# Paged attention with a conditional residual on one Trainium2 core: value rows gathered raw and masked on the way into the operand, a fixed opening, and loads in written order

## The chip, the cores and the metric

The kernel runs on one NeuronCore of a Trainium2 chip. The metric is device time in microseconds. It was run three times; the median counts. Beside that, one execution was taken by the hardware profiler, and all readings of engines, waits and transfers come from it.

Five engines work side by side: TensorE (matrix products), VectorE, ScalarE (activations), GpSimd, and SyncE (SP), which here only issues transfers. Each works through its own queue of instructions in order, and semaphores between them carry the dependencies.

## The reference, cut to what matters

```python
# B=64 sequences, S=32 new tokens each, HID=512; D=128, HQ=32 query heads, HK=8 key heads
# 64 pages of 32 keys; 16 pages to a sequence, so L=512 cached positions
x = x + einsum('bct,bcd->bdt', x, L0_weights[cond])        # 32x32 mix picked per sequence
q, k, v = x @ Wq.T, x @ Wk.T, x @ Wv.T
q = rope(rmsnorm(q, q_norm_w), pos); k = rope(rmsnorm(k, k_norm_w), pos)
# pos = cache_seqlens[:, None] + arange(S)
kc = k_cache[block_table]; vc = v_cache[block_table]       # 16 pages in a table's order
k_all, v_all = concat([kc, k]), concat([vc, v])            # 512 cached + 32 new
valid = concat([arange(512) < cache_seqlens, ones(32)])
scores = where(valid, q @ k_all.T / sqrt(D), -1e30)        # 4 query heads share a key head
o = softmax(scores) @ v_all
x = x + o @ Wo.T
```

All of it is float32.

## The kernel before, in words

**Tiling.** A step is a tile of 128 tokens, that is BT = 4 sequences (batches) of 32 tokens. There are 16 steps to a half of the heads (`hh`: 4 key heads, 16 query heads) and two halves, so 32 steps. Within a step there are 16 slots, one for each batch and key head (`slot = bt * GH + g`). In a slot TensorE makes `scores` (four matmuls: 512 cached keys x 128 queries, transposed, so that keys lie on partitions), ScalarE takes exp of them into `pr` without a maximum, and one slot later TensorE makes `values` from `pr` and the value operand `v_t`. That operand has a 129th column of ones for the denominator: a masked position has a zero row there, 129th column included, so masking needs no work on the scores. The new tokens' own keys come in `new_scores` and `new_values` once a step. `turn` transposes a finished batch, and `out_proj` of a step runs in slot 3 of the following one.

**The next step's preparation.** In the slots of one step the next step's tile is prepared by a table of pieces: x with its mix (`x1_a`), its transpose (`x1_b`), the projections of k, v and four groups of q (`k_a`, `v_a`, `q_a`; a projection is four float32 matmuls 512 wide, and `norm_rope` follows on ScalarE, VectorE and GpSimd) and the transposes of the results (`k_b`, `q_b`). They lie in slots 0, 2, 4, 5, 6, ... 15.

**Cached keys.** `load_k` fetches the 16 pages of a batch by 16 transfers on SP, 1 MB in all, two batches ahead; `head_keys` copies one head's keys out of it on VectorE, one batch ahead.

**Cached values.** A table `v_tab` in device memory is built for each half: `table_piece` reads 128 rows of the cache, sets the column of ones and writes 129 columns for each head; a last row is zero. Then `load_v` gathers rows from the table straight into `v_t` (two buffers, `v_bufs`), four gathers of 128 rows to a batch, where `v_idx` points a masked position at the zero row. Only the first four batches (`DIRECT`) are gathered raw and masked by VectorE (L326). The first table is built before the loop, the second in steps 4 to 11.

**Order.** Nearly all of the order is left to a planner, which takes instructions by priority of writing as their operands become ready by its own estimate; so an engine's queue may differ from the order of the source. `tc.issue_after` and `tc.manual_schedule` are the means to fix an order: the first puts instructions behind a given one on its engine, the second keeps the written order for the engines named (all, when none is named).

**Opening.** Weights and Wo are issued on ScalarE's queue; the tables of sine and cosine are made first for one tile (`tables_a`), then for the other 15 in two goes (`tables_b`, `angles`). The main loop follows.

At the end the kernel counts denominators outside a safe range; when there is one, a second, exact version runs (`run(True)`). It did not run here.

Of the kernel before, what the change touches and what calls it, by code (L numbers as in the profile page):

```python
# [48 lines left out]
PIECES = PAGES * PSIZE // P  # L49
ZROW = PAGES * PSIZE  # L50
DIRECT = BT
# [4 lines left out]
def cond_resid_paged_attention_kernel(  # L56
# [29 lines left out]

    cond_sb = const.tile([P, NT], I32, tag="cond", name="cond_sb")
    nc.sync.dma_start(cond_sb, cond)
    pages_sb = const.tile([B, NPP], I32, tag="pages", name="pages_sb")
    nc.sync.dma_start(pages_sb, pages)  # L90
    pages_v_sb = const.tile([P, B * VC], I32, tag="pages_v", name="pages_v_sb")
    nc.sync.dma_start(pages_v_sb, pages_v)
    lens_sb = const.tile([P, NT], I32, tag="lens", name="lens_sb")
    nc.sync.dma_start(lens_sb, lens)
    lens_all_i = const.tile([P, B], I32, tag="lens_all_i", name="lens_all_i")
    nc.sync.dma_start(lens_all_i, lens_row.partition_broadcast(P))

    part_i = const.tile([P, 1], I32, tag="part_i", name="part_i")
    nc.gpsimd.iota(part_i, pattern=[[0, 1]], base=0, channel_multiplier=1)
    row_i = const.tile([P, 1], I32, tag="row_i", name="row_i")  # L100
    nc.vector.tensor_scalar(row_i, part_i, S - 1, None, ALU.bitwise_and)
    row = const.tile([P, 1], F32, tag="row", name="row")
    nc.vector.tensor_copy(row, row_i)
    part = const.tile([P, 1], F32, tag="part", name="part")
    nc.vector.tensor_copy(part, part_i)

    cond_idx = const.tile([P, NT], I32, tag="cond_idx", name="cond_idx")
    nc.vector.tensor_scalar(cond_idx, cond_sb, float(S), row, ALU.mult, ALU.add)

    ident = const.tile([P, P], F32, tag="ident", name="ident")  # L110
    make_identity(nc, ident)


    v_idx = const.tile([P, B, VC], I32, tag="v_idx", name="v_idx")
# [3 lines left out]
    norm_w = {}  # L118
    for name, src in (("q", qn_w), ("k", kn_w)):
        w = const.tile([P, D], F32, tag=f"norm_{name}", name=f"norm_{name}")  # L120
        norm_w[name] = w, src
    freq = const.tile([P, HD], F32, tag="freq", name="freq")
# [8 lines left out]
    def angles(t0, t1, tmp):  # L131

        n = (t1 - t0) * HD
        ang, turns, red = (tmp[:, i, 0:n] for i in range(3))
        for t in range(t0, t1):
            nc.vector.tensor_scalar(
                ang[:, (t - t0) * HD : (t - t0 + 1) * HD],
                freq,
                pos[:, t : t + 1],
                None,  # L140
                ALU.mult,
            )
# [16 lines left out]
    def tables_a(tmp):  # L159

        for name in norm_w:
            w, src = norm_w[name]
            nc.sync.dma_start(w, src.partition_broadcast(P))
            norm_w[name] = w
        nc.sync.dma_start(freq, inv_freq.partition_broadcast(P))
        nc.vector.memset(half_pi, math.pi / 2)
        nc.vector.memset(minus_half, -0.5)
        nc.vector.tensor_copy(pos, lens_sb)
        nc.vector.tensor_scalar(pos, pos, row, None, ALU.add)
        angles(0, 1, tmp)  # L170

    def gather_rows(at):
        nc.vector.tensor_copy(lens_all, lens_all_i)
        for c in range(VC):
            key = const.tile([P, 1], F32, tag=f"key{c}", name=f"key{c}")
            nc.vector.tensor_scalar_add(key, part, float(c * P))
            nc.vector.tensor_scalar(valid[:, :, c], lens_all, key, None, ALU.is_gt)
        row2 = const.tile([P, 1], F32, tag="row2", name="row2")
        nc.vector.tensor_scalar(row2, row, float(NHH), None, ALU.mult)
        nc.vector.tensor_scalar(  # L180
            v_row, pages_v_sb, float(PSIZE * NHH), row2, ALU.mult, ALU.add
        )
        past = const.tile([P, 1], F32, tag="past", name="past")
        nc.vector.tensor_scalar_add(past, row, -float(ZROW))
        nc.vector.tensor_scalar(at, pages_v_sb, float(PSIZE), past, ALU.mult, ALU.add)
        nc.vector.tensor_tensor(at, at, valid.rearrange("p b c -> p (b c)"), ALU.mult)
        nc.vector.tensor_scalar_add(
            v_idx.rearrange("p b c -> p (b c)"), at, float(ZROW)
        )

    def tables_b(kv):

        for t0, t1 in ((1, NT // 2), (NT // 2, NT)):
            angles(t0, t1, kv.tile([P, 3, 8 * HD], F32, tag="k_t", name=f"trig{t0}"))
# [3 lines left out]
    ]  # L198
    v_tab = [
        dram.tile([ZROW + 1, GH * (D + 1)], F32, tag=f"v_tab{hh}", name=f"v_tab{hh}")  # L200
        for hh in range(NHH)
# [8 lines left out]
    def steps_of(exact, pools):  # L210
# [31 lines left out]


        wt = {}

        def load_w(kind, hh, g=0, eng=None):
# [10 lines left out]
            if kind == "o" and not exact:  # L257
                src = src.rearrange("(h j p) e -> h p j e", h=REP, p=S)
                for h in range(REP):
                    (eng or nc.gpsimd).dma_start(t[h * S : (h + 1) * S, :, :], src[h])  # L260
                return
            (eng or nc.gpsimd).dma_start(t, src.rearrange("(c p) e -> p c e", p=P))

        def load_cond_weights(t):
            w_sel = work.tile([P, S], F32, tag="w_sel", name=f"w_sel_{t}_{uid}")
# [8 lines left out]
        def load_x(t):  # L274
            xt = work.tile([P, HID], F32, tag="acc", name=f"xt_{t}_{uid}", bufs=3)
            nc.sync.dma_start(xt, x[t * P : (t + 1) * P, :])
            return xt, load_cond_weights(t)
# [3 lines left out]
        def load_k(hh, b):  # L281
            k_raw = kv.tile([P, NPP, GH, PSIZE], F32, tag="k_t", name=f"k_t_{hh}_{b}_{uid}")

            with ExitStack() as order:
                if last_k:
                    order.enter_context(tc.issue_after(last_k[0]))
# [15 lines left out]
        def load_v(hh, b):  # L302
            v_t = v_bufs[b % 2]
            if exact or hh or b >= DIRECT:
                for c in range(VC):
                    nc.gpsimd.indirect_dma_start(  # L306
                        out=v_t[:, c, :, :].rearrange("p g d -> p (g d)"),
                        out_offset=None,
                        in_=v_tab[hh],
                        in_offset=bass.IndirectOffsetOnAxis(  # L310
                            ap=v_idx[:, b, c : c + 1], axis=0
                        ),
                    )
                return v_t
            raw = wpool.tile([P, VC, GH * D], F32, tag="wo3", name=f"raw_{b}")
            for c in range(VC):
                nc.gpsimd.indirect_dma_start(
                    out=raw[:, c, :],
                    out_offset=None,
                    in_=vc,  # L320
                    in_offset=bass.IndirectOffsetOnAxis(
                        ap=v_row[:, b * VC + c : b * VC + c + 1], axis=0
                    ),
                )
                ok = valid[:, b, c : c + 1]
                nc.vector.tensor_scalar(  # L326
                    v_t[:, c, :, 0:D],
                    raw[:, c, :].rearrange("p (g d) -> p g d", g=GH),
                    ok,
                    None,  # L330
                    ALU.mult,
                )
# [405 lines left out]
        for g in range(GH):  # L738
            load_w("q", 0, g, eng=nc.scalar)
# [157 lines left out]
```

## Time and profile before

| | |
|---|---|
| time, median of 3 | 2466.02 us (2464.14 to 2476.43) |
| profiled execution, span | 2339.8 us |
| granted TensorE clock, mean | 0.986 |
| transfers | 335.94 MB, mean 144 GB/s |
| landing of a gathered value chunk (256 KB), median | 4.5 us |
| exp of one slot on ScalarE, x512 | 597 ns |
| masked copy on VectorE (first four batches), x16 | 480 ns |
| gather issue on GpSimd, x496 | 1137 ns |

How to read it: the timed runs and the profiled execution are measured apart and differ by a constant-looking 125 us, so a timed run is compared with a timed run and a span with a span. "Busy" of TensorE is the modelled time of pipelined matmuls. Clock is the share of full speed that was granted to TensorE[...]. An instruction's line is the line in the listing above.

### The profile page before, as it was taken

To read this page: it belongs to the slowest core of one execution; us is meant where nothing else is said; L and a number is where in the kernel's file an instruction comes from. 1 tells how busy PE (TensorE), PEld (TensorE's weight loads), DVE (VectorE), ACT (ScalarE), POOL (GpSimd) and SP (SyncE) were. 2 spreads that over 40 slices of the span, in tenths; PEclk is the share of its full clock that TensorE was granted. 3 is DMA by queue.
4 is the path that set the end of the run, shared out by engine and by line. 5 is a ranking of instruction groups with operands and counts; after the bars stand their busy time and mean duration, and the time that the engine had idled before them with its cause. 6 is when DMAs were issued, how large, how long until landed. Compare 5 with 4: busy or idle time off the path is not lost.

```text
span 2339.8 us, 41048 instructions
## 1 busy us (share of the span) xinstructions
PE 2229.0 (95%) x13538; PEld 1565.5 (67%) x13538; DVE 1075.7 (46%) x2800; ACT 611.5 (26%) x1180; POOL 848.4 (36%) x963
## 2 busy tenths in 40 slices
PE   3789999999999999999998999999999999999997
PEld 1466666776666776667775667766667776667775
DVE  4444444554444554444552444544444554444452
ACT  1222222222222322222321222322222232222231
POOL 3133333443333443333443333433333443334341
PEclk8889999999999999999999999999999999999999
DMA  8564555544444544454847355544454544445442
GB/s 255 154 183 139 168 166 166 160 117 122 136 133 141 143 116 122 132 141 136 252 127 195 105 146 144 141 120 124 134 145 141 144 132 121 134 128 149 141 133 60
DMA packets 381155, 335.94 MB, mean 144 GB/s; under 512 B 45186, under 2 KB 324354, under 8 KB 380932
## 3 DMA queue, kind: packets, MB, share of 16 engines
q1 hardware_dynamic: 331332, 176.72, 26.1%
q0 software_dynamic: 44704, 147.07, 22.6%
q10 hardware_dynamic: 4896, 9.44, 1.3%
q8 instruction: 108, 1.77, 0.3%
q14 instruction: 115, 0.94, 0.1%
HBM read 312.00 MB, written 21.04 MB: 142 GB/s over the span
## 4 chain that ended last, share of the span: by engine, by line
PE 84%; DMA 5%; DVE 4%; POOL 4%; ACT 1%; issue 1%; SPq 1%; ACTq 0%; DVEq 0%; POOLq 0%
PE pout_x L504 19%; PE pp_q_x L423 18%; PE po_x L617 16%; PE ps_x L559 15%; PE pp_v_x L423 4%; PE pp_k_x L423 4%; PE pt_q_x L467 2%; POOL v_x L306 2%; PE pnv_x L601 2%; DMA tab<-in_vc_dram 2%; DMA v_tab<-tab 1%; POOL rs_q_x L440 1%; PE psn_x L577 1%; DVE rope_q_x L459 1%; DVE ms_q_x L437 1%
## 5 line engine op out<-in xcount | busy, mean ns | idle before, releaser
L306 POOL DMA_INDIRECT v_x<-v_tab,v_idx x496 | 563.9, 1137 | 969.0 <-PE po_x L617 856.8
L617 PEld LDWEIGHTS po_x<-v_x,pr_x 128*128 128x128 f32 x4096 | 518.0, 192 | 124.4 <-issue 113.4
L567 ACT ACTIVATE pr_x<-ps_x 128x512 f32<-128x512 f32 x512 | 305.9, 597 | 1040.2 <-PE ps_x L559 1004.5
L559 PE MATMUL ps_x<-qt_x,kh_x 128*128 128x128 f32 x4096 | 543.0, 276 | 14.5 <-ACT qt_x L494 14.5
L617 PE MATMUL po_x<-v_x,pr_x 128*128 128x129 f32 x4096 | 551.0, 277 | 4.1 <-DMA v_x<-v_tab,v_idx 4.1
L559 PEld LDWEIGHTS ps_x<-qt_x,kh_x 128*128 128x128 f32 x4096 | 500.9, 193 | 15.9 <-ACT qt_x L494 15.3
L423 PE MATMUL pp_q_x<-wq_x,x1t_x 128*128 128x512 f32 x1024 | 466.3, 599 | 0.0
L504 PE MATMUL pout_x<-wo_x,ot_x 128*128 128x512 f32 x1024 | 444.9, 592 | 2.2 <-DVE ot_x L642 2.2
L504 PEld LDWEIGHTS pout_x<-wo_x,ot_x 128*128 128x128 f32 x1024 | 192.1, 190 | 232.0 <-issue 229.6
L423 PEld LDWEIGHTS pp_q_x<-wq_x,x1t_x 128*128 128x128 f32 x1024 | 187.3, 193 | 187.9 <-issue 187.9
L552 DVE COPY kh_x<-k_t_x 128x512 f32<-128x512 f32 x512 | 217.2, 425 | 111.9 <-PE ps_x L559 64.1
L437 DVE TENSOR_REDUCE ms_q_x<-sq_q_x 128x4 f32<-128x512 f32 x128 | 87.7, 685 | 318.2 <-ACT sq_q_x L433 318.1
L440 POOL TENSOR_TENSOR rs_q_x<-ms_q_x,minus_half 128x4 f32<-128x4 f32 x128 | 132.9, 1039 | 221.6 <-DVE ms_q_x L438 220.3
L433 ACT ACTIVATE sq_q_x<-pp_q_x 128x512 f32<-128x512 f32 x128 | 76.4, 597 | 379.5 <-PE pp_q_x L423 362.5
L629 DVE TENSOR_TENSOR nv_x<-po_x,nv_x 128x258 f32<-128x258 f32 x256 | 105.9, 414 | 87.8 <-PE po_x L617 87.5
L459 DVE TENSOR_TENSOR rope_q_x<-rope_q_x,rs_q_x 128x512 f32<-128x512 f32 x128 | 88.0, 688 | 102.4 <-POOL rs_q_x L440 101.7
L423 PE MATMUL pp_k_x<-wk_x,x1t_x 128*128 128x512 f32 x256 | 117.6, 603 | 2.0 <-ACT x1t_x L389 2.0
L423 PE MATMUL pp_v_x<-wv_x,x1t_x 128*128 128x512 f32 x256 | 115.2, 592 | 0.0
L632 DVE TENSOR_TENSOR o_x<-nv_x,rden 128x256 f32<-128x256 f32 x256 | 107.5, 420 | 2.4
L511 DVE TENSOR_TENSOR xt_x<-pout_x,xt_x 128x512 f32<-128x512 f32 x16 | 11.1, 691 | 210.1 <-PE pout_x L504 210.1
L511 DVE TENSOR_TENSOR acc_x<-pout_x,acc_x 128x512 f32<-128x512 f32 x16 | 11.1, 691 | 209.8 <-PE pout_x L504 209.8
L467 PE MATMUL pt_q_x<-ident,rope_q_x 128*128 128x128 f32 x512 | 79.4, 278 | 25.7 <-DVE rope_q_x L459 25.6
(99 smaller groups left out, 1388.7 us busy)
## 6 DMA issues: line engine op xcount, KB each, us to landing
k_t_x<-in_kt_dram SPq DMA_DIRECT2D x2048, 64.0 KB
v_tab<-tab SPq DMA_DIRECT2D x32, 258.0 KB
tab<-in_vc_dram SPq DMA_DIRECT2D x32, 256.0 KB
v_x<-v_tab,v_idx POOLq DMA_INDIRECT x496, 4.5
wo_x<-in_wo_dram POOLq DMA_DIRECT2D x20, 256.0 KB, 10.0
xt_x<-in_x_dram SPq DMA_DIRECT2D x16, 256.0 KB
wq_x<-in_wq_dram ACTq DMA_DIRECT2D x4, 1024.0 KB
x1t_d<-x1t_x SPq DMA_DIRECT2D x16, 256.0 KB
```

What stands on the lines that cost most here:

```text
L306: nc.gpsimd.indirect_dma_start(out=v_t[:, c, :, :].rearrange("p g d -> p (g d)"), out_offset=None, in_=v_tab[hh], in_offset=bass.IndirectO ...
L423: nc.tensor.matmul(pp, st.x1t[:, c, :], w[:, c, :], start=(c == 0), stop=(c == KC - 1))
L437: nc.vector.tensor_reduce(ms, sq, AX.X, ALU.add)
L440: nc.gpsimd.tensor_tensor(rs, ms, minus_half, ALU.pow)
L459: nc.vector.tensor_tensor(rd, rd, rs.unsqueeze(2).to_broadcast([P, 4, D]), ALU.mult)
L467: nc.tensor.transpose(pt[:, h, :], rd[:, h, :], ident)
L504: nc.tensor.matmul(po, st.ot[:, i, :], wt["o", st.hh, i // 4][:, i % 4, :], start=(i == 0), stop=(i == QH - 1),)
L552: nc.vector.tensor_copy(k, ba.k_raw[:, :, g, :])
L559: nc.tensor.matmul(ps[:, c, :], ba.k[g][:, c * P : (c + 1) * P], queries(ba, g), start=True, stop=True,)
L567: nc.scalar.activation(pr, ps, AF.Exp, scale=SCALE)
L617: nc.tensor.matmul(ba.po[:, g % 2, :], ba.pr[g][:, c, :], ba.v_t[:, c, g, :], start=(c == 0), stop=(c == VC - 1),)
L632: nc.vector.tensor_tensor(ba.o[:, both, :], t[:, :, 0:D], rd.unsqueeze(2).to_broadcast([P, 2, D]), ALU.mult,)
```

## The change

What it does:

1. The value table, its pieces, its zero row and `v_idx` go. Every batch's values are gathered raw from the cache (`fetch_v`, 128 rows x 512 into one of RAW = 3 chunk buffers), and ScalarE copies each chunk into the operand with the validity of each row as its scale (`mask_v`); GpSimd writes the 129th columns (`mask_ones`). Three chunks of the batch after next are fetched at the end of a batch, the fourth when the first has been copied. For the second half `other_half` shifts all row numbers by one.
2. The opening is written out by hand for all engines, up to the end of the first batch: weights on SP in the order of their use, matmuls that keep TensorE busy while it waits (`keep_warm`), small trig tables of two tiles, key copies on ScalarE, the second step's x and v brought forward.
3. SP keeps the written order throughout. Weights, Wo and the accumulator's store (`store`, now in slot 5) are placed by hand; x1t is stored from ScalarE's queue.
4. The other trig tables are made two tiles at a time in slot 3 of steps 1 to 6, behind the last key copy and the last exp.
5. The pieces move to slots 0, 3, 4 (two projections), 5, 6, 8, 10 and 13.

It is for a shorter opening, for less traffic in device memory, and for an order that doesn't hang on the planner's estimates. The core of the diff:

```diff
-PIECES = PAGES * PSIZE // P
-ZROW = PAGES * PSIZE
-DIRECT = BT
+RAW = 3
+WARM = 24
+TRIG = 2
...
+    whole.enter_context(tc.manual_schedule(engines={mybir.EngineType.SP}))
+    opening.enter_context(tc.manual_schedule())
...
+    def other_half(by):
+        nc.gpsimd.tensor_scalar(v_row, v_row, by, None, ALU.add)
...
-                    (eng or nc.gpsimd).dma_start(t[h * S : (h + 1) * S, :, :], src[h])
+                    nc.sync.dma_start(t[h * S : (h + 1) * S, :, :], src[h])
...
-        def load_v(hh, b):
...
-        def table_piece(hh, i):
...
+        def fetch_v(b, c):
+            raw = work.tile([P, GH, D], F32, tag="raw", name=f"raw_{b}_{c}_{uid}", bufs=RAW)
+            nc.gpsimd.indirect_dma_start(
+                out=raw.rearrange("p g d -> p (g d)"),
+                out_offset=None,
+                in_=vc,
+                in_offset=bass.IndirectOffsetOnAxis(
+                    ap=v_row[:, b * VC + c : b * VC + c + 1], axis=0
+                ),
+            )
+            return raw
+
+        def mask_v(b, c, raw):
+            ok = valid[:, b, c : c + 1]
+            nc.scalar.activation(v_bufs[b % 2][:, c, :, 0:D], raw, AF.Copy, scale=ok)
+
+        def mask_ones(b):
+            nc.gpsimd.tensor_copy(
+                v_bufs[b % 2][:, :, :, D], valid[:, b, :].unsqueeze(2).to_broadcast([P, VC, GH])
+            )
...
-            nc.sync.dma_start(x1t_d[st.t], st.x1t.rearrange("p c q -> p (c q)"))
+            nc.scalar.dma_start(x1t_d[st.t], st.x1t.rearrange("p c q -> p (c q)"))
...
+        load_w("q", 0, 0)
+        load_w("k", 0)
+        load_w("q", 0, 1)
+        batch = Batch(first, 0)
+        load_w("q", 0, 2)
+        load_w("v", 0)
+        load_w("q", 0, 3)
+        x_second = load_x(1)
+        later = Batch(first, 1)
...
+        keep_warm(WARM)
...
+        angles(0, trig)
+        x1_a(first, mix=False)
+        x1_c(first)
...
+        for c in range(RAW):
+            batch.fetch(c)
+        q_a(first, 0)
+        k_a(first)
+        for g in range(GH):
+            head_keys(batch, g, nc.scalar)
+        q_a(first, 1)
+        q_b(first, 0)
+        scores(batch, 0)
+        batch.fill(0)
+        batch.fetch(3)
...
+            do = {
+                0: (x1_a,),
+                3: (x1_b,),
+                4: (k_a, (q_a, 0)),
+                5: ((q_a, 1),),
+                6: (v_a, k_b, (q_b, 0)),
+                8: ((q_a, 2), (q_b, 1)),
+                10: ((q_a, 3), (q_b, 2)),
+                13: ((q_b, 3),),
+            }
...
+                    if slot == 3:
                         out_proj(steps[st.n - 1])
+                        if st.n + 1 < NT // TRIG:
...
+                            with tc.issue_after(last["dve"]), tc.issue_after(last["act"]):
+                                angles((st.n + 1) * TRIG, tmp)
+                    if slot == 5 and st.n:
+                        store(steps[st.n - 1])
...
+                    if st.n == 0 and 5 <= slot < 9 or st.n == NT and slot >= 12:
+                        load_w("o", st.hh, (slot - 5 if st.n == 0 else slot - 12))
+                    if st.t == NT - 2 and st.hh + 1 < NHH:
+                        if slot == 11:
+                            load_w("k", st.hh + 1)
+                            load_w("v", st.hh + 1)
+                        if slot in (12, 13):
+                            for i in range(2):
+                                load_w("q", st.hh + 1, 2 * (slot - 12) + i)
...
                         head_keys(later, g)
                         if g == 2:
-                            later.load_values()
...
+                            later.fill(0)
+                            later.fetch(3)
+                            for c in range(1, VC):
+                                later.fill(c)
+                            mask_ones(later.b)
...
+                    for c in range(RAW):
+                        later.fetch(c)
```

## The prediction, made before the changed kernel was seen on the chip

> **What bounds the kernel now.** I read four views: the page, TensorE's timeline over the first 180 us, the chain of waits over one step in the middle, and the busy time in short stretches of that step. The page first (engine busy times; busy tenths in 40 slices of 58.5 us; granted clock; the chain that ended last):
>
> ```profile
> PE 2229.0 (95%) x13538; PEld 1565.5 (67%) x13538; DVE 1075.7 (46%) x2800; ACT 611.5 (26%) x1180; POOL 848.4 (36%) x963
> ...
> PE   3789999999999999999998999999999999999997
> ...
> PEclk8889999999999999999999999999999999999999
> ...
> PE 84%; DMA 5%; DVE 4%; POOL 4%; ACT 1%; issue 1%; SPq 1%; ACTq 0%; DVEq 0%; POOLq 0%
> ```
>
> TensorE is the bound everywhere but in the first three slices, one slice in the middle and the last. ScalarE has 74% of the span free. Next TensorE's timeline of the opening (start, duration, operation; in brackets the idle time before it and what ended it) and one line of ScalarE's queue:
>
> ```profile
> 18.50 2.05 PE L377 MATMUL pmix_x<-xt_x,bd_x 128*128 128x512 f32 x2 [18.50 <-DVE bd_x L375]
> 29.12 6.04 PE L423 MATMUL pp_k_x<-wk_x,x1t_x 128*128 128x512 f32 x8 [2.01 <-ACT x1t_x L389]
> 50.14 1.11 PE L467 MATMUL pt_k_x<-ident,rope_k_x 128*128 128x128 f32 x4 [11.54 <-DVE rope_k_x L459]
> 79.50 2.08 PE L559 MATMUL ps_x<-qt_x,kh_x 128*128 128x128 f32 x8 [14.49 <-ACT qt_x L494]
> 153.02 0.86 PE L467 MATMUL pt_q_x<-ident,rope_q_x 128*128 128x128 f32 x4 [4.89 <-DVE rope_q_x L459]
> ...
> 60.63 17.64 ACTq L260 DMA_DIRECT2D wo_x<-in_wo_dram  x5
> ```
>
> The first projection starts at 29.1 us at half clock (6.04 us against 3.60 us later); then VectorE makes the trig tables of 15 tiles between the parts of k's rope, and ScalarE stands 17.6 us in its own issues of Wo, behind which the copy of qt waits. The first out-projection starts at 174.9 us. I count the TensorE work done by then with steady durations: two sets of projections (6 x 3.44 + 5 x 0.44 + x1 1.4 = 24.3 us each), 20 scores of 0.89, 19 values of 0.89, own keys twice 2.6, one x1 of 1.4: 90 us. So the opening loses about **85 us**.
>
> After it, steps are even: the out-projections lie 70.53 us apart in the first half and 68.77 in the second. The idle gaps in such a step are 0.54 us (last q transpose behind its rope) and, in the first half, 0.44 us (px1t behind the ScalarE copy of pnv); the work is thus 69.55 and 68.24 us, 2205 us for 32 steps. At the change of halves one gap is 9.53 us (VectorE stuck 8.9 us on a key load). The tail after the last out-projection is 11 us.
>
> Three more answers: two short stretches of a step (length, then busy time of TensorE, weight loads, VectorE, ScalarE, GpSimd; clock, DMA share, GB/s), then waits (total us, times, longest), then the landing of one gathered chunk:
>
> ```profile
> 657.00:659.00 2.00, 1.46 (x14) 1.26 (x13) 1.18 (x3) 0.60 (x1) 1.81 (x2) 1.00 0.98 292
> 669.00:671.00 2.00, 2.00 (x20) 2.00 (x19) 0.67 (x3) 0.89 (x3) 0.95 (x1) 1.00 1.01 317
> ```
>
> ```profile
> ACT pr_x L567 <- PE ps_x L559: 1004.5, 475, 15.2
> POOL v_x L306 <- PE po_x L617: 856.8, 121, 23.3
> DVE kh_x L552 <- DMA k_t_x<-in_kt_dram: 21.7, 9, 8.9
> ```
>
> ```profile
> DMA to landing us min/median/max: 3.1/4.5/6.3
> ```
>
> ScalarE and GpSimd wait for TensorE, not the other way round. But in the run of slots without a projection (652 to 671 us) the DMA engines are full at about 300 GB/s.
>
> **What the Trainium skill says.** (1) *ScalarE: Activation LUTs*, What ACT_TABLE_LOAD costs: an ACTIVATE takes 186 ns + 0.833 ns an element, 93 ns more for a per-partition pointer operand. For 512 elements that is 613 ns; the trace has 597 for the exp. With valid as a pointer scale my estimate of a masked copy is 0.70 us. (2) *DMA: Bandwidth & Descriptors*, Anatomy of one DMA: about 2.0 us plus bytes over 436 GB/s, 2.6 us for a 256 KB chunk. The trace says 4.5 in the median; I use 4.5. (3) Same page, Issuing engines are not separate DMA queues: moving loads to SP gains no bandwidth, only sequencer time. The trace agrees: loads from three engines fill the DMA at 0.96 and 297 GB/s between 10 and 20 us. (4) *TensorE: Matmul & The Clock Gate*, Why this matters for your kernels: busy some 4 us to reach the full clock, no gaps beyond about 3 us. The trace agrees: clock 0.54 between 40 and 50 us after a gap.
>
> **The change part by part.**
>
> *Opening.* New chain to the first projection: cond is the first load on SP; in the trace nothing tells its landing, since VectorE sat behind lens_sb until 9.1 us. Bounds 3 and 9 us; I take 3.5, as the big loads no longer go first. Index 0.6, gather issue 1.1, landing 4 to 7 (w_sel took 3.9 in the median, 7 in the loaded opening; I take 5.5), bd 0.9, pmix 1.0 warm, add 0.7, px1t 0.5, copy 0.6: first projection at 14.5 us instead of 29. The 24 warming matmuls lie in the wait. After that the written order alternates a projection (3.44) with the rope of one before it. VectorE has 3.4 us a rope (0.69+0.60+0.09+0.66+0.60+0.70), 17 us for five, plus some 7 for two small trig tables, rows and masks: less than TensorE's 38 us of work in this stretch. The 15-tile tables go (the rest is made two tiles a step beside the 13.7 us out-projection, table switches too), Wo leaves ScalarE's queue, and the 4 MB read and 4 MB write of the first value table go, some 28 us of DMA at 290 GB/s. For waits on ropes, key loads (now queued behind weights on SP) and Wo I put 10 us. Loss 25 us, bounds 15 and 45. **Gain 60 (40 to 70).**
>
> *Masked copies and gathers, steady.* 512 x 0.70 = 358 us more on ScalarE, 611 to about 970 of 2290: 42%, hidden as a sum. As a queue it is not: an exp must be done one slot after its scores, and in a bare slot that leaves 1.78 - 0.75 = 1.0 us. One masked copy fits; two in a row cost 0.4. The fourth chunk is fetched only after the first is copied (1.0 issue, 4.5 landing); if its copy stands in ScalarE's queue before it has landed, the exp behind it waits, then values on TensorE. In two batches of four a projection (3.44) covers that; in two it doesn't. Also the eight copies of pnv (0.30 each) share slots 0 to 2 with masked copies. And the bare run grows by two slots (3.6 us), so the key load of the next batch but one (16 issues, 8 to 9 us) lands 1 to 2 us after VectorE wants it. Together I take 0.8 us a step, bounds 0 and 4: +24 us over 30 steps. Against that the new slots give every q transpose at least two slots after its projection and px1t a full slot: the gaps of 0.54 and 0.44 go, 15 x 0.98 + 15 x 0.53 = -23. **Net 0.**
>
> *Half change.* K/V/Q weights are loaded on SP from step 14 on, ahead of key loads in the same queue: 6 MB take 20 us and may hold VectorE's key copies as now. Change 0, bounds -9 and +9. Wo of the second half comes in slots 12 to 15 of step 16, inside the full DMA stretch, 4 MB or 14 us for use 13 us later: +4, bounds 0 and 10.
>
> *No cost:* table pieces of half two (DMA not full there), mask_ones on GpSimd (64% idle), the half's row shift (once), later stores (SP waits, keys have 22 us).
>
> Sum: -60 + 0 + 0 + 4 = -56 us. The timed runs stand 125 us above the profiled execution of 2341.6; nothing on the page says why, and I carry it over: 2466 - 56 = **2410 us**, a span near 2284.
>
> **The rivals.**
> 1. *Clean steady state*: no new waits, the gaps gone, 2466 - 60 - 23 = 2383. For: ScalarE 74% free, waits all on TensorE. Against: one-slot margin of 1.0 us.
> 2. *The opening is bound by its loads*: 6 MB weights, 2 MB keys, 1.8 MB values, then 4 MB Wo on one queue, 14 MB in 48 us. Loss 60, gain 25, plus 4 and some steady cost: 2450. For: DMA share 0.8 to 0.96 in the first 40 us now. Against: the written order loads in order of use.
> 3. *ScalarE becomes the wait* (the other side): two batches of four stall 2 us for the fourth chunk, 4 us a step, 30 steps, +120: 2466 - 60 + 4 + 120 - 23 = 2507. For: in the opening VectorE's masked copies waited 13.4 us for raw chunks in 5 of 16 cases, up to 6.8. Against: the landing spread is only 3.1 to 6.3 in the steady state, and the values are needed a batch later.
>
> **How the numbers follow.** Forecast 0.48, rival 1 0.20, rival 2 0.16, rival 3 0.16. Faster by 0.5% means under 2453.7: the first two and over half of the third, 0.78. Same 0.08, from rival 2 and mild forms of 3; slower 0.14. Range 2370 (rival 1 with an opening loss of 15) to 2475 (a mild rival 3).
>
> **What would show it.** Right: first projection near 15 us, first out-projection near 115, steps of 68 to 71 us, masked copies near 0.70 us without idle before most exps other than on TensorE. Wrong: steps over 72 us with TensorE's values waiting for the exp (pr), and the exp or the masked copy for raw; or TensorE idle on key copies in the first 100 us.

## The result, and the profile after

| | before | after |
|---|---|---|
| time, median of 4 runs | 2465.49 us (2464.14 to 2476.43) | 2375.47 us (2373.59 to 2378.08) |
| ratio | | 0.9626, 95% interval 0.9597 to 0.9655 |
| profiled execution, span | 2339.8 (shown above), 2463.2 (a second one, of the unchanged kernel) | 2374.6 |
| transfers | 335.94 MB | 318.14 MB |

The change makes the kernel 3.7% faster. But one row upsets the reading of the profile above: every timed run of the kernel before beside these took over 2464 us, and so did a second profile of it. The profile that the prediction rests on, with its own time of 2341.55 us, belongs to another population. The last experiments show which: **the chips differ**. On the chip of the first eight experiments (A) the kernel before takes 2465 to 2484 us; on the two chips of the last four (B and C) it takes 2338 to 2347 us. The first profile fits B and C to a few microseconds, the timed runs and the result fit A. No record says which chip took the first profile or the result, so this is inferred from the times. A drift with time instead of a difference of chips is unlikely: the first profile, the earliest of all, is fast, and A was slow in both of its sessions. But A was not tried again at the end.

The page of the second profile of before (chip A): engine busy, then two groups of instructions, with the mean of one in ns, and the idle time before them with what ended most of it.

```profile
PE 2298.7 (93%) x13538; PEld 1619.5 (66%) x13538; DVE 1078.2 (44%) x2800; ACT 621.2 (25%) x1180; POOL 846.3 (34%) x963
...
L601 PE MATMUL pnv_x<-vn_x,pn_x 32*128 32x129 f32 x1024 | 87.5, 322 | 54.3 <-ACT nv_x L609 35.3
...
L609 ACT COPY nv_x<-pnv_x 128x258 f32<-128x258 f32 x256 | 82.7, 383 | 119.1 <-remote 64.9
```

The page of after: engine busy, clock in tenths, then the gathers, the values and the masked copies.

```profile
PE 2273.7 (96%) x13606; PEld 1597.2 (67%) x13606; DVE 1103.6 (46%) x2780; ACT 936.5 (39%) x1726; POOL 814.5 (34%) x1032
...
PEclk9999999999999999999999999999999999999998
...
L287 POOL DMA_INDIRECT raw_x<-in_vc_dram,v_row x512 | 530.8, 1037 | 297.2 <-ACT v_x L300 167.3
L582 PE MATMUL po_x<-v_x,pr_x 128*128 128x129 f32 x4096 | 563.6, 280 | 47.9 <-ACT pr_x L532 28.6
...
L300 ACT ACTIVATE v_x<-raw_x,valid 128x512 f32<-128x512 f32 x512 | 342.6, 717 | 241.6 <-DMA raw_x<-in_vc_dram,v_row 218.2
```

Read the last three together: the masked copy takes 717 ns, ScalarE stands 218.2 us before such copies for a chunk that has not landed, and TensorE's values wait 28.6 us for the exp that is queued behind.

TensorE's timeline of after at the start: the first projection is at 13.8 us (29.1 in the profile above), behind the warming matmuls.

```profile
1.54 8.25 PE L716 MATMUL warm<-ident 128*128 128x128 f32 x48 [1.54 <-POOL ident masks.py:199]
10.23 1.10 PE L337 MATMUL pmix_x<-xt_x,bd_x 128*128 128x512 f32 x2 [0.44 <-issue]
...
13.83 3.65 PE L381 MATMUL pp_q_x<-wq_x,x1t_x 128*128 128x512 f32 x8
17.32 3.60 PE L381 MATMUL pp_k_x<-wk_x,x1t_x 128*128 128x512 f32 x8
```

The spans, cut at the starts of out-projections (OP 0 to OP 31, read from TensorE's timeline). The left half is chip A, before against after (whose chip is inferred). The right half is the first profile of before against a kernel on chip C that differs from after only in the place of three gathers, plus four that nothing reads (the last experiment).

| stretch | before, A | after | gain | before, first profile | nearly after, C | gain |
|---|---|---|---|---|---|---|
| start to OP 0 | 175.0 | 130.5 | 44.5 | 174.8 | 130.2 | 44.6 |
| OP 0 to 13 (first half) | 986.6 | 959.1 | 27.5 | 919.3 | 932.2 | -12.9 |
| OP 13 to 18 (halves change) | 371.6 | 367.2 | 4.4 | 355.7 | 366.5 | -10.8 |
| OP 18 to 30 (second half) | 863.4 | 843.5 | 19.9 | 825.2 | 839.5 | -14.3 |
| OP 30 to the end | 66.6 | 74.3 | -7.7 | 64.8 | 73.2 | -8.4 |
| span | 2463.2 | 2374.6 | 88.6 | 2339.8 | 2341.6 | -1.8 |

The first cut does not fall at the same place of the work. At OP 0 before has done 20 slots of scores and 18 of values, after only 16 and 16 (matmuls counted in the traces); at the 0.89 us of a slot's scores or values the six that are missing are 5.3 us, which after does in its first step. At OP 1 both have done the same: there the changed kernel is 37.2 us ahead without the stall of chip A (208.5 on C against 245.8 in the first profile) and 43.1 on A (209.1 against 252.3). So the opening is worth some 39 us (44.5 - 5.3), and the row of the first half is 5.3 us better than it looks.

The rest is decided later: the steps and the change of halves give 57 us more on A, and on C they and the end take 41 us back. The spans of the right half are single executions; the one on C was the slowest of its 11 runs.

### Where a step loses time on chip A

The loss lies in slots 1 and 2, while four gathers of values run on GpSimd and 16 key-page transfers are issued on SP. Busy time in four microseconds of that place (length; TensorE, weight loads, VectorE, ScalarE, GpSimd; clock, DMA share, GB/s), for the second profile of before:

```profile
473.00:474.00 1.00, 0.35 (x4) 0.15 (x2) 0.00 (x0) 0.01 (x1) 0.69 (x2) 1.00 0.78 159
474.00:475.00 1.00, 0.48 (x2) 0.29 (x2) 0.00 (x0) 0.37 (x1) 0.70 (x2) 1.00 1.01 345
475.00:476.00 1.00, 0.14 (x1) 0.14 (x2) 0.00 (x0) 0.37 (x1) 0.68 (x1) 1.00 0.92 290
476.00:477.00 1.00, 0.35 (x2) 0.15 (x2) 0.00 (x0) 0.14 (x1) 0.00 (x0) 1.00 0.91 307
```

The same place of the same program in the first profile:

```profile
454.00:455.00 1.00, 1.00 (x12) 0.88 (x10) 1.00 (x3) 0.77 (x3) 0.94 (x1) 1.00 0.84 280
455.00:456.00 1.00, 1.00 (x17) 1.00 (x16) 0.48 (x2) 0.94 (x3) 0.72 (x1) 1.00 0.76 167
456.00:457.00 1.00, 0.74 (x7) 0.55 (x7) 0.00 (x0) 0.97 (x4) 0.70 (x2) 1.00 1.08 360
457.00:458.00 1.00, 1.00 (x12) 1.00 (x11) 0.00 (x0) 0.73 (x2) 0.53 (x1) 1.00 0.89 272
```

The traffic is alike (159 to 345 GB/s against 167 to 360). On A TensorE, VectorE and ScalarE all stand nearly still; in the other profile TensorE and ScalarE go on. After such a stall TensorE's clock is halved for one or two windows of 3.4 us: 24 half-clock stretches in the second profile of before (143.8 us in all), 6 in the first (68.8 us).

Now after, on GpSimd and TensorE, in a step with the stall. The gathers follow each other 0.30 us apart, five in a row (w_sel, the conditioning weights of a later step, is among them):

```profile
635.11 0.98 POOL L287 DMA_INDIRECT raw_x<-in_vc_dram,v_row  x1 [0.53 <-ACT v_x L300]
636.40 0.95 POOL L287 DMA_INDIRECT raw_x<-in_vc_dram,v_row  x1 [0.30 <-issue]
637.65 0.94 POOL L287 DMA_INDIRECT raw_x<-in_vc_dram,v_row  x1 [0.30 <-issue]
638.89 0.94 POOL L248 DMA_INDIRECT w_sel_x<-in_w_cond_dram,cond_idx  x1 [0.30 <-DMA raw_x<-in_vc_dram,v_row]
640.14 0.95 POOL L287 DMA_INDIRECT raw_x<-in_vc_dram,v_row  x1 [0.30 <-issue]
```

```profile
640.78 0.37 PE L582 MATMUL po_x<-v_x,pr_x 128*128 128x129 f32 x1 [0.45 <-issue]
642.18 1.03 PE L582 MATMUL po_x<-v_x,pr_x 128*128 128x129 f32 x4 [1.04 <-issue]
643.01 1.92 PE L524 MATMUL ps_x<-qt_x,kh_x 128*128 128x128 f32 x8
```

"issue" means that the profile shows nothing that TensorE waited for; single matmuls go out with a microsecond between them. The next scores take 1.92 us instead of 1.06, at half clock. In steps 2 to 6 of after no run of five occurs: the small trig tables are made there in one of the raw buffers, and a pause of 0.9 to 2.1 us parts the run.

I sorted the steps of all traces by the longest run of gathers in these slots (0.6 us or less between them) and by the time from the step's own scores (`psn`) to its out-projection, without the first step, those around the change of halves, and the kernel without copies below, whose values wait for landings:

| longest run | chip A: median (range), steps | B, C and the first profile |
|---|---|---|
| five, first half | 15.4 us (13.3 to 16.7), 47 | 9.9 us (9.5 to 10.5), 12 |
| four, first half | 13.7 us (11.3 to 15.9), 15 | 10.5 us (9.9 to 11.7), 13 |
| three or fewer, first half | 11.4 us (9.8 to 14.3), 34 | 10.1 us (9.5 to 11.8), 35 |
| four, second half | 10.6 us (9.4 to 13.0), 25 | 8.2 us (8.2 to 8.2), 22 |
| five, second half | none | 8.6 us (8.4 to 9.0), 4 |
| three or fewer, second half | 9.3 us (8.2 to 13.1), 71 | 8.2 us (8.2 to 11.0), 34 |

On A the median step is the longer, the longer its run, though the ranges overlap; elsewhere the run costs half a microsecond at most. The kernel before has runs of five and four. Three raw buffers make runs of three, because the fourth chunk waits for a copy; but where a gather of w_sel fills that pause, as in steps 7 to 12 of after, the run is five again.

### The profile page after: what moved, and what is told of

Its sections match the earlier page's. It is cut to its first block, busy times and chain, and to the rows that moved or that the text cites. A ratio compares the mean times of both kernels' runs of the same rounds, so it can differ in the third digit from the quotient of the medians.

```text
span 2374.6 us, 42146 instructions
## 1 busy us (share of the span) xinstructions
PE 2273.7 (96%) x13606; PEld 1597.2 (67%) x13606; DVE 1103.6 (46%) x2780; ACT 936.5 (39%) x1726; POOL 814.5 (34%) x1032
## 2 busy tenths in 40 slices
DMA packets 362471, 318.14 MB, mean 134 GB/s; under 512 B 44160, under 2 KB 306944, under 8 KB 362240
## 3 DMA queue, kind: packets, MB, share of 16 engines
q1 hardware_dynamic: 317520, 176.31, 25.6%
## 4 chain that ended last, share of the span: by engine, by line
PE 88%; DMA 5%; issue 3%; ACT 2%; POOL 1%; DVE 1%; another core or an unknown queue 0%; SPq 0%; ACTq 0%; POOLq 0%; DVEq 0%
PE pout_x L463 19%; PE po_x L582 19%; PE pp_q_x L381 17%; PE ps_x L524 17%; PE pp_v_x L381 4%; PE pp_k_x L381 4%; DMA raw_x<-in_vc_dram,v_row 4%; PE pnv_x L566 2%; PE pt_q_x L425 2%; PE psn_x L542 1%; ACT pr_x L532 1%; PE pmix_x L337 1%; PE pt_k_x L425 1%; ACT v_x L300 1%; DMA wq_x<-in_wq_dram 0%
## 5 line engine op out<-in xcount | busy, mean ns | idle before, releaser
L287 POOL DMA_INDIRECT raw_x<-in_vc_dram,v_row x512 | 530.8, 1037 | 297.2 <-ACT v_x L300 167.3
L582 PE MATMUL po_x<-v_x,pr_x 128*128 128x129 f32 x4096 | 563.6, 280 | 47.9 <-ACT pr_x L532 28.6
L524 PE MATMUL ps_x<-qt_x,kh_x 128*128 128x128 f32 x4096 | 550.8, 278 | 7.8 <-ACT qt_x L453 4.2
L524 PEld LDWEIGHTS ps_x<-qt_x,kh_x 128*128 128x128 f32 x4096 | 508.0, 195 | 12.2 <-ACT qt_x L453 5.1
L300 ACT ACTIVATE v_x<-raw_x,valid 128x512 f32<-128x512 f32 x512 | 342.6, 717 | 241.6 <-DMA raw_x<-in_vc_dram,v_row 218.2
L517 DVE COPY kh_x<-k_t_x 128x512 f32<-128x512 f32 x506 | 224.5, 448 | 200.4 <-PE ps_x L524 77.2
L370 POOL TENSOR_TENSOR cw_k_x<-norm_k,cos 128x64 f32<-128x64 f32 x32 | 10.1, 316 | 584.1 <-DVE ms_k_x L396 584.1
L303 POOL COPY v_x<-valid 128x16 f32<-128x16 f32 x128 | 29.7, 232 | 476.5 <-PE po_x L582 476.5
L391 ACT ACTIVATE sq_q_x<-pp_q_x 128x512 f32<-128x512 f32 x128 | 75.8, 592 | 210.3 <-PE pp_q_x L381 196.4
L398 POOL TENSOR_TENSOR rs_q_x<-ms_q_x,minus_half 128x4 f32<-128x4 f32 x128 | 144.7, 1131 | 20.5 <-DVE ms_q_x L396 17.3
L402 DVE TENSOR_TENSOR rope_q_x<-pp_q_x,cw_q_x 128x512 f32<-128x512 f32 x128 | 87.4, 682 | 73.3 <-PE pt_k_x L425 71.5
```

Source lines behind the costliest of these rows:

```text
L287: nc.gpsimd.indirect_dma_start(out=raw.rearrange("p g d -> p (g d)"), out_offset=None, in_=vc, in_offset=bass.IndirectOffsetOnAxis(ap=v_ro ...
L300: nc.scalar.activation(v_bufs[b % 2][:, c, :, 0:D], raw, AF.Copy, scale=ok)
L398: nc.gpsimd.tensor_tensor(rs, ms, minus_half, ALU.pow)
L402: nc.vector.tensor_tensor(r.rearrange("p h e f -> p h (e f)"), pp.rearrange("p (h d) -> p h d", h=4), cw.rearrange("p e f -> p (e f)").uns ...
L517: last["dve"] = nc.vector.tensor_copy(k, ba.k_raw[:, :, g, :]).ins
L524: nc.tensor.matmul(ps[:, c, :], ba.k[g][:, c * P : (c + 1) * P], queries(ba, g), start=True, stop=True,)
```

## The experiments

The first experiment was made under two theories (their letters have nothing to do with the chips): A, the extra of the timed runs is constant and lies outside what the profile shows; B, it lies in the steps, which run in two forms. All ratios are against the kernel before on the same chip.

**The kernel before again.** No edit.

> The kernel before, unchanged. Its timed runs gave 2464 to 2476 us, its profiled execution 2340. Theory A (the timed runs carry some fixed extra that the profile lacks): the profiled execution is near 2340 again and the timed ones near 2465. Theory B (the kernel before has two forms of running, one of which has some 4 us more in every step, with TensorE's clock lowered again and again): a profiled execution near 2465 with steps of 74 to 75 us instead of 70.5 and 68.8, and clock windows of one half in most of them.

Measured: 2471.13 us (2464.98 to 2478.46, 12 runs), a span of 2463.2, steps of 76.3 and 77.3 us in turn where the first profile has 70.5. The extra is in the steps. So the first profile is no reference for the result, and the prediction's carried-over 125 us was wrong in kind.

**The opening left to the planner.**

```diff
-    opening.enter_context(tc.manual_schedule())
...
-        opening.close()
```

> The changed kernel, with the opening's order left to the planner as the rest is. If the hand-written order of the opening brings the gain, the first out-projection starts some 20 to 45 us later and the time is 2395 to 2420. If the gain comes from the smaller work of the opening (no tables for 15 tiles, no Wo on ScalarE's queue), under 10 us are lost: 2376 to 2386.

Measured: 2382.8 us, ratio 0.9634 (0.9609 to 0.966); first out-projection at 128.8 us against 130.5. The ratio is that of after (0.9626) within its interval: holding the written order adds nothing that can be measured, and the opening is short without it (at OP 0 as much work is done as in after).

**Masked copies on VectorE.**

```diff
-            nc.scalar.activation(v_bufs[b % 2][:, c, :, 0:D], raw, AF.Copy, scale=ok)
+            nc.vector.tensor_scalar(v_bufs[b % 2][:, c, :, 0:D], raw, ok, None, ALU.mult)
```

> The changed kernel, with the masked copies on VectorE (480 ns each in the kernel before) instead of ScalarE. If the exps wait behind the masked copies and TensorE behind the exps (about 1 us a step in the trace), the waits of values on pr go and the steps fall toward 69.6 and 68.2 us: 2330 to 2355. If VectorE, which now waits for the fourth chunk, becomes the wait for ropes, key copies and po: 2380 to 2450.

Measured: 2395.3 us, ratio 0.9687 (0.966 to 0.9713). The values' wait for pr falls from 28.6 to 1.5 us, so it does come from the copies in ScalarE's queue; but new waits come up (28.7 us of `pnv` for ScalarE's copies of nv), and the ratio is worse than 0.9626. ScalarE is the better place.

**No copies at all.**

```diff
-            raw = work.tile([P, GH, D], F32, tag="raw", name=f"raw_{b}_{c}_{uid}", bufs=RAW)
+            raw = v_bufs[b % 2][:, c, 0 : GH * D]
...
```

> The changed kernel without masked copies: chunks are gathered straight into the operand, whose rows are unmasked and whose denominators are the next head's first value; masking and denominators are left out. It shows what the copies cost. If the copies and the wait for the fourth chunk make the losses of a step: steps near 69.6 and 68.2 us, 2320 to 2345. If they are hidden and the losses come from keys or the bare run of slots: within 10 us of the changed kernel, 2366 to 2385.

Measured: 2734.32 us, ratio 1.1053. The values wait 257 us in 201 places for landings. This took away more than the copies: without raw buffers a gather can only start when TensorE has read the operand. As a price of the copies it is inconclusive; it shows what the lookahead is worth.

**The value path alone**, in the kernel before: `fetch_v`, `mask_v`, `mask_ones` and three raw buffers in place of `load_v` and `table_piece`; opening, slots and queues as before. To make room, four small tiles share buffers.

> The kernel before with the value path of the change alone: raw gathers into three chunk buffers, masked copies by ScalarE, ones by GpSimd, no tables of values and no table pieces; the pieces stay in their old slots, the opening and all loads stay in the planner's order, Wo is still loaded from ScalarE's queue, the trig tables of 15 tiles are still made in the opening. Theory V (the steps became shorter because the values' gathers no longer wait for TensorE's last read of the operand): steps fall from 76.3/77.3 us to 72 to 74, some 40 us of the 92 come with it, and the first out-projection stays near 165 to 175 us: 2420 to 2440 us. Rival S (the steps became shorter through the moved pieces and the written order): steps stay at 76 to 77 and the time at 2455 to 2475 us; with the copies in the queue of the exp it may even be slower, to 2490.

Measured: 2419.62 us (2417.82 to 2422.09), ratio 0.9784 (0.9768 to 0.9801). The first out-projection comes at 152.5 us, with the same work done as in before: 22.5 us, over half of the opening's gain. What gives the other half (the small trig tables, the queue of Wo, the loads on SP, the warming matmuls) was not tried one by one. In the second half twelve steps take 842.7 us against 863.4, all of the change's gain there; in the first half nothing is gained (990.0 against 986.6). There one step is short, 72.95 us between neighbours of 77.45 and 76.35: it is the one whose run of gathers is parted, by a wait of 2.1 us.

**The pieces back in their old slots**, in after.

```diff
-                4: (k_a, (q_a, 0)),
-                5: ((q_a, 1),),
-                6: (v_a, k_b, (q_b, 0)),
+                4: (k_a,),
+                5: (v_a,),
+                6: ((q_a, 0),),
...
```

> The changed kernel with the pieces of a step back in the slots of the kernel before (13 slots with one piece each; the short last slots are 14 and 15 only). Theory V: the steps stay within 1 us of the changed kernel's; the gaps behind the ropes come back (some 0.5 to 1 us a step, 15 to 30 us in all): 2385 to 2405 us. Rival S: the steps go back to 76 to 77 us in the first half and the time rises by 40 us or more, to 2415 or over.

Measured: 2399.97 us (2393.56 to 2408.78), ratio 0.9716 (0.9694 to 0.9737). Thirteen steps of the first half take 986.9 us against 959.1 of after, the second half is like after's (837.0 against 843.5). So on A the moved pieces, beside the new value path, are worth 28 us in the first half, and the value path alone 21 in the second. The moved pieces without the value path were not tried. Neither theory put it so: each gave all to one of the two.

**Half of the key bytes**, in before.

```diff
-            for j in range(NPP):
+            for j in range(NPP // 2):
                 ins = nc.sync.dma_start(
...
```

> The kernel before with half of the key loads: 8 of the 16 pages of each batch are loaded, and the copy of a head's keys repeats those eight for the other eight (the same copy time, other scores). It takes 67 MB and 1024 issues out. Theory D (the long steps of the kernel before come from the stretch in which the key loads and the four gathers of values fill the DMA engines: all queues are slow together there for some 3 us, and TensorE's clock is halved after it): with half the key bytes the stall and most of the half-clock windows go (from 24 to under 10), and the steps fall from 76.3/77.3 to 70 to 72 us; the time falls by 80 to 120 us, to 2350 to 2390. Rival (the long steps have nothing to do with DMA traffic, but with TensorE's waits at the short slots or the clock alone): steps stay over 75 us, time over 2450.

Measured: 2426.66 us (2422.45 to 2427.7), ratio 0.9808 (0.9791 to 0.9824). The first steps still take 75.4 to 77.0 us, with 19 half-clock stretches. Theory D expected 70 to 72: it falls as an account of the bulk; half the bytes and half the issues take 0.7 us off a step of the first half and 1.4 off one of the second.

**Half of the gathered bytes**, in after.

```diff
-                out=raw.rearrange("p g d -> p (g d)"),
+                out=raw[:, 0 : GH // 2, :].rearrange("p g d -> p (g d)"),
...
```

> The changed kernel with gathers of half a row (256 of 512 elements; the masked copy reads that half twice, so its length is the same, and the values are others). It takes 67 MB out. Theory D: the stalls that are left in steps 5 to 10 of the first half go, steps 71 us or less throughout, time 2330 to 2355 us. Rival (what is left over 71 us is not DMA traffic): steps and time within 10 us of the changed kernel's 2375 to 2385.

Measured: 2383.03 us (2376.13 to 2386.15), ratio 0.9631 (0.9609 to 0.9652), with steps of 74.7 to 75.7 us where after has 74.4 to 75.8. The bytes gathered don't matter for the long steps. With the one before, this led to theory R: it is the run of gathers that counts.

**w_sel out of the run**, in after, then in before. In after:

```diff
+                    if slot == 11 and 0 < st.n and st.n + 2 < NT:
+                        with tc.issue_after(last["pool"]):
+                            x_next = x_next, load_cond_weights(st.n + 2)
...
-                        x_next = load_x(st.n + 2), load_cond_weights(st.n + 2)
+                        x_next = load_x(st.n + 2)
```

> The changed kernel with the gather of the conditioning weights (w_sel of the step after next) queued on GpSimd behind the last norm of the step (slot 11 and later) instead of between the gathers of values in slots 1 and 2. Theory R (what makes steps long is an unbroken run of gathers on GpSimd, 0.30 us apart, beside the 16 key-page issues on SP: all queues stall there, and the longer the run, the longer the stall): runs of five in steps 7 to 12 become runs of three or four, so these six steps fall from 75.1 to 71 to 72.5 us: time 2350 to 2365 us against 2375 to 2385. Rival C (the runs are only a companion; the long steps come from the clock or from time): no change, 2375 to 2385.

> The kernel before with the gather of w_sel queued behind the last norm of the step in the same way; nothing else is changed. Theory R: the runs of five in the first nine steps become runs of four, as in its second half, where a step has a stall of 2.7 us (71.5 against 68.8): steps fall from 76.3/77.3 to 73 to 74.7 us: time 2435 to 2455 us against 2473. Rival C: no change.

**A pause in the run**, in before: w_sel late, and between the second and third gather of a batch four short memsets:

```diff
+                        if c == 2 and not exact:
+                            order.enter_context(tc.issue_after(pause(ins)))
...
```

> The kernel before with w_sel queued late and with four short memsets of a spare tile by GpSimd (0.2 us each) between the second and the third gather of each batch: only extra work, no transfer less, no wait less. Theory R: no run is longer than two, the stalls go, and the steps come to 70.5 to 71.5 in the first half and 68.8 to 69.5 in the second: time 2340 to 2365 us against 2473. Rival C, or a theory in which the bytes in flight are what counts: steps stay at 74 or more in the first half, time over 2430.

Measured, all three on chip B, where the kernel before takes 2342.93 us (2338.45 to 2347.29, 22 runs): 2338.04, ratio 0.9979 (0.9968 to 0.9991); 2352.09, ratio 1.0037 (1.0021 to 1.0053); 2346.33, ratio 1.0013 (1.0003 to 1.0024). There was no stall to take away on this chip, so they say nothing on theory R. The first is after in all but the place of one gather, and gains 4.9 us on B. They show what the measures cost where they cure nothing: w_sel late in before adds 9 us, with 9.2 us of idle time before `pmix`; w_sel late and the pauses together cost 1.1 us a step in the first half (`pmix` waits 23.3 us for GpSimd) and give 0.76 in the second.

**Both cases in one execution**, in after: w_sel late for the last three, and an extra gather of it in steps 22 to 25.

```diff
+LATE = range(11, 14)
+EXTRA = range(22, 26)
...
```

> The changed kernel with two blocks of steps altered, so that one execution holds both cases: in the first half the last three gathers of w_sel are queued late (steps 10 to 12 lose their run of five, steps 7 to 9 keep it), and in four steps of the second half (22 to 25) a gather of w_sel that nothing reads is put between the gathers of values, so that their runs grow from three to four or five. Theory R on a chip where the kernel before takes about 2470 us: steps 7 to 9 take about 75 us and steps 10 to 12 71 to 72.5; steps 22 to 25 take 73 to 75.5 us between neighbours of 70 to 71; the time is 2375 to 2392. Rival T (long steps belong to a stretch of time or of the program, runs only go along): steps 10 to 12 stay at 75, steps 22 to 25 at 70 to 71. On a chip where the kernel before takes about 2343 us neither block should show (steps of 70.5 to 72 and 69 to 70.5 throughout), and the time is that of the changed kernel on such a chip within a few us: 2330 to 2345, a ratio of 0.994 to 1.001, if the change gives little there.

Measured on chip C: 2338.27 us (2332.26 to 2343.43, 11 runs) against 2342.53 (2337.99 to 2347.48, 16 runs), ratio 0.9975 (0.9964 to 0.9987). Its GpSimd and TensorE with a run of five:

```profile
628.28 0.98 POOL L289 DMA_INDIRECT raw_x<-in_vc_dram,v_row  x1 [0.54 <-ACT v_x L302]
629.57 1.15 POOL L289 DMA_INDIRECT raw_x<-in_vc_dram,v_row  x1 [0.30 <-ACT pr_x L534]
631.02 1.19 POOL L289 DMA_INDIRECT raw_x<-in_vc_dram,v_row  x1 [0.31 <-ACT nv_x L576]
632.52 0.94 POOL L250 DMA_INDIRECT w_sel_x<-in_w_cond_dram,cond_idx  x1 [0.30 <-issue]
633.76 0.95 POOL L289 DMA_INDIRECT raw_x<-in_vc_dram,v_row  x1 [0.30 <-ACT nv_x L576]
```

```profile
630.86 1.09 PE L568 MATMUL pnv_x<-vn_x,pn_x 32*128 32x129 f32 x16
631.88 1.16 PE L584 MATMUL po_x<-v_x,pr_x 128*128 128x129 f32 x8
632.88 1.06 PE L526 MATMUL ps_x<-qt_x,kh_x 128*128 128x128 f32 x8
633.77 0.60 PE L347 MATMUL px1t_x<-ident,xt_x 128*128 128x128 f32 x4
```

The same run, and TensorE goes through without a gap. Steps with the extra gather take 69.4 to 70.0 us like their neighbours. As was expected for such a chip, neither block shows, and 0.9975 is what nearly the whole change is worth there. In its list of waits, TensorE's side reads (us in total, times, longest):

```profile
PE po_x L584 <- ACT pr_x L534: 38.5, 33, 3.5
PE pt_q_x L427 <- DVE rope_q_x L419: 5.2, 3, 3.9
```

**Left open.** That breaking the runs shortens the steps on A rests on the table of steps, on one step of an experiment and on two kernels whose runs became shorter for other reasons. No kernel that changes only the run has been on chip A, so there it is a correlation; in the kernel with half of the gathered bytes, two of the steps with w_sel in their run reach only four and take 13.7 and 14.0 us, those with five 14.0 to 14.4. Nor is it known what differs between the chips, what stops three engines at once, or what the change itself, to the letter, gives on B and C.

## Why the prediction was partly right

Direction and range hold; the sum came out from terms that don't. That the time fell into the range of 2370 to 2475 us is in good part luck: without the stall of chip A, which the profile read for the prediction doesn't contain, a nearly identical kernel gains only 4.3 us (on C).

- **Start of the opening: right.** First projection predicted at 14.5 us, measured 13.8; `pmix` at 10.2.
- **Gain of the opening: 60 predicted, some 39 measured**, just under its bounds of 40 to 70. The loss was put at 25 us, bounds 15 and 45. At OP 0, at 130.5 us, the work done is by the prediction's own prices 90 - 4 x 0.89 - 3 x 0.89 = 84 us, so the loss is 47. The term that was too small is "For waits on ropes, key loads (now queued behind weights on SP) and Wo I put 10 us". After the first projection TensorE idles 20.7 us up to the first out-projection. The largest two waits are 3.96 us for the residual add and 3.95 for a rope; the second comes from the masked copies: ScalarE stood 7.15 us for a chunk before the copy at 76.59 us, and the square of k, from which VectorE's next ropes follow, stood behind that copy in its queue (77.22). By my estimate 9 us more go to half clock, half of the 18.5 us that TensorE is busy in such windows.
- **The masked copy: right.** 0.70 us predicted, 717 ns measured.
- **Steps, the waits added: right in kind and nearly in size.** "Together I take 0.8 us a step": in the two stretches of steps on C (25 steps) TensorE's values stand 25.6 us, 1.0 a step; over the whole span they wait 38.5 us for pr on C and 28.6 in after. The mechanism is the one named: an exp stands behind a masked copy that itself stands for its chunk, as the page's 218.2 us show.
- **Steps, the gaps removed: right where the first profile applies.** -23 predicted. After OP 0 the q transposes wait 16.1 us in the first profile and 0.6 on C, those of `px1t` 5.0 and 2.5: 18.0 together.
- **"Net 0" for the steps: wrong on both kinds of chip.** With the 5.3 us of work set right, the two stretches are 21.9 us longer than in the first profile (12.9 + 14.3 - 5.3), and on A 52.7 shorter (27.5 + 19.9 + 5.3). Of the 21.9, 11 are idle time of TensorE and some 4 half clock; the other 7 are not explained. The gain on A comes from the stall.
- **Half change: 0 and +4 predicted** within bounds of -9 to +9 and 0 to 10; -4.4 on A, +10.8 on C. **The end** was given no term and costs 7.7 to 8.4 us more. Some 6 us of it lie behind the last computing instruction (16.3 us from the issue of the last store to the end, 10.3 in before on A); why was not looked into.
- **"nothing on the page says why, and I carry it over": the step that failed.** The 125 us are no constant. A second profile of the same kernel has them in its steps: on A the kernel before pays 123.4 us more than in the first profile (2463.2 - 2339.8), but after only 33.0 more than its near twin on C (2374.6 - 2341.6). So the change takes away some 90 us of what the prediction took for fixed. Steps, half change and end together gain 49.4 us on A (88.6 - 39.2) and lose 41.0 on C (-1.8 - 39.2). On a chip like that of the profile the forecast of a gain of 56 us would have been wrong: the near twin gains 4.3 us there (2342.53 - 2338.27).
- **Rivals.** The first, at 2383, came nearest in number but not in reason: there are new waits, and the opening gained less than it assumed. The second put the opening's loss at 60 because it is bound by its loads; the 47 measured lie between that and the forecast's 25, and in the chain through the first 131 us of after landings of raw chunks make up 19 us and one of Wq 9.7, so it was right in part. The third, ScalarE as the wait, is real at 28.6 to 38.5 us, far from its 120.

## What to carry to other kernels

When a profile's own time and the timed runs differ by five per cent, take the profile again before any step of it is priced, and ask whether both come from one chip. A version that wins 3.7% on one chip may win 0.25% on the next, so a change is best timed on more than one. A copy put into the queue of the exp is cheap by its sum and still costs about a microsecond a step when its chunk may land late; and an opening can be shortened by what it leaves out without its order being held by hand. Before two traces are cut at one event, count what work each has done by then.

## What the hardware showed unexpectedly

- The same program takes 2465 to 2484 us on one chip and 2338 to 2347 on two others. Most of it lies in slots 1 and 2 of the steps: 76.3 and 77.3 us a step against 70.5 in most of the first half, some 71.5 against 68.8 in the second, with similar traffic in flight.
- In the stall on chip A two engines advance in beats: ScalarE's copies of nv start at 637.15, 637.88 and 638.60 us in after, 0.72 us apart, and in the second profile of before TensorE's pairs of `pnv` start at 474.42, 475.86 and 477.29, two such beats apart.
- In these traces the half-clock stretches last 3.41 us or whole multiples of it (6.83, 10.24; the last of a trace is cut off by its end), and in the long steps of chip A they start 75.09 or 78.51 us apart, 22 or 23 times 3.41. The steps of before alternate between 76.3 and 77.3 us, together 45 such windows. Whether the windows set the length of the steps or only follow it is not shown.
